# Three kinds of work change hands around the graphs that run ahead: row sums to a tile of their own, two evictions to ScalarE, half of the copies to VectorE

## The chip, the cores and the metric

The kernel runs on one core of a Trainium2 chip. A core has five engines with an instruction queue each: TensorE (PE in the profile, PEld for its weight loads), VectorE (DVE), ScalarE (ACT), GpSimd (POOL) and SyncE (SP), which here only issues transfers. Each queue is worked off in order, and engines wait for each other by semaphores. The metric is the device time of one execution in microseconds. Before the change it was 2126.53 us (median of 4 runs, 2122.99 to 2128.66).

## The reference, cut to what matters

There are 64 graphs of 256 nodes with 256 features, and two layers. What each computes:

```python
# layer 0, for each graph
deg = adjacency_matrix.sum(axis=-1);  deg = where(deg != 0, deg, 1.0)
a_plus = deg**-0.5 [:, None] * adjacency_matrix * deg**-0.5 [None, :] + max(alpha, 1e-10) * eye
x = layernorm(x + (a_plus @ x) @ W.T + b)
# layer 1, for each graph
h = relu(bn(conv1d(x.T, conv1_w, 0)))
h = bn(conv1d(h, conv2_w, 8))            # 17 taps along the nodes
x_conv = relu(h + x.T).T
s = x @ w_se.T + b_se                    # 3 numbers per node
dist = |s_n|^2 + |s_m|^2 - 2 s_n . s_m;  A = exp(-dist) * mask   # mask is adj
x_nmp = A @ relu(x @ w_msg.T + b_msg)
gi = concat(x_conv, x_nmp) @ w_ih.T + b_ih;  gh = x @ w_hh.T + b_hh
r, z = sigmoid(gi_r + gh_r), sigmoid(gi_z + gh_z);  n = tanh(gi_n + r * gh_n)
x = layernorm(x + (1 - z) * n + z * x)
```

Everything is float32.

## The kernel before, in words

The 64 graphs are worked in 4 groups (Q = 16 graphs each). For each group there are three kinds of work.

The **graph stages**: `layer0(g)` computes the first layer of a graph, and `layer1(g)` its second layer up to the gates. In `layer0`, `degrees()` (lines 354 to 359) sums the rows of the adjacency tile `a_t` on ScalarE: an activation that copies `a_t` and leaves the row sum in `deg` as accumulator output. The copy itself is not used. It is written into the tile `adjT`, which line 379 then overwrites with the transposed adjacency. From `deg`, VectorE and GpSimd make `dis` (power -1/2, line 369), ScalarE scales x with it into `x1` (line 391), and two VectorE operations put the diagonal into `adjT` (line 381). `adjT` has 3 buffers, and a buffer is free again when the multiplication at line 508 of three graphs before has read it.

`x1_transposed(g)` transposes x1 by TensorE into a PSUM bank and evicts it into `xn`: VectorE takes the first half (line 430, with a scale and a bias per partition, which put ones into the place of one channel), ScalarE the second (line 431). `layer1` multiplies it with the first convolution's weights (`p_conv`, line 446). ScalarE evicts that into `h` and `scols`, then come `p_msg` (467), the transform of h along the nodes (`p_dft`, 482, evicted into the tile V of all graphs of a group, line 487), the transposed distance columns `p_rows` (495), evicted as `dist_l` by ScalarE (497) and `dist_r` by VectorE (499), the distances `p_dist` (506), their exponential (507, ScalarE), the product with adjT (508, VectorE) and `p_nmp` (515). TensorE's order in a graph's turn is `p_rows`, `p_hT` of layer 0 two graphs ahead (399), `p_dist`, `p_out` (409), the transposes for the next graph's `xn`, `p_nmp`, then the next graph's `p_conv`, `p_adjT` (378), `p_msg` and `p_dft`.

The **convolution of a group** in the frequency domain: `products` (line 541, TensorE, weights streamed from memory) and then the inverse transform, `real_transform`, `complex_begin` and `complex_end`, all on VectorE, in place in the tile V/M; its results leave by the transfers of line 729.

The **gates** of a group's graphs: `gru(g)` (`p_g`, line 856), with their inputs loaded back from memory into tiles of the pool `gate`.

The groups overlap. While TensorE multiplies and VectorE transforms group 0, the first 12 graphs of group 1 (16 to 27) are already worked: AHEAD is 12, and the set ALONE holds exactly these graphs, beside which no gates run. For graphs in ALONE the transposes of the next graph's x1 are issued early, ahead of `p_nmp` (lines 510 and 511). The tile V is still in use then, so their transforms go into a second tile, V2. When `complex_end` has finished and its results have left, `copies` (lines 1080 to 1087) brings each graph's part from V2 to V, one copy of 128 x 768 elements per graph, on ScalarE. Then V2's memory is given back and the pool `gate` opens. For groups 1 and 2 AHEAD is 6, and gates of the group before run beside the graphs.

What comes before what on a queue is decided by a scheduler at build time, from the order in which the program issues the work and from the dependencies; `paced` ties steps of the VectorE transform to marked instructions of the graphs.

Of the kernel before, what the change touches and what calls it, by code (L numbers as in the profile page):

```python
# [9 lines left out]
F32 = mybir.dt.float32  # L10
AF = mybir.ActivationFunctionType
ALU = mybir.AluOpType
AX = mybir.AxisListType

P = 128
# [11 lines left out]
def kernel(  # L27
# [27 lines left out]
    nc = tc.nc  # L55
    B, N, D = x.shape
# [8 lines left out]
    GT = N // NT  # L65
# [6 lines left out]
    const = ctx.enter_context(tc.tile_pool(name="const", bufs=1))  # L72
# [9 lines left out]
    def bank(name):  # L82
        return ps.tile([P, 512], F32, tag="bank", name=name)
# [7 lines left out]
    def mark(op, gates=0):  # L91
        marks.append((op.ins, gates))
# [24 lines left out]
    alpha_t = const.tile([P, 1], F32)  # L117

    vectors = const.tile([16, P], F32, name="bn_in")
    neg_half = const.tile([P, 4], F32)  # L120
    nc.vector.memset(neg_half, -0.5)
    load(0)
# [17 lines left out]
    unit, others_only = ident[:, 0:1], const.tile([P, 1], F32, name="others_only")  # L140
# [177 lines left out]
    def layernorm(y, eps=LN_EPS):  # L318

        chunks = range(y.shape[1])  # L320
        st = small.tile([P, NCH, nc.vector.BN_STATS_DIM], F32, name="ln_st")
        mv = small.tile([P, NCH, nc.vector.BN_AGGR_DIM], F32, name="ln_mv")
        rs = small.tile([P, NCH], F32, name="ln_rs")
        for c in chunks:
            nc.vector.bn_stats(st[:, c, :], y[:, c, :])  # L325
            nc.vector.bn_aggr(mv[:, c, :], st[:, c, :])
        nc.vector.tensor_scalar(rs[:, : len(chunks)], mv[:, : len(chunks), 1], eps, None, op0=ALU.add)  # L327
        nc.gpsimd.tensor_tensor(rs[:, : len(chunks)], rs[:, : len(chunks)], neg_half[:, : len(chunks)], op=ALU.pow)  # L328
        yield
        mr = small.tile([P, NCH], F32, name="ln_mr")  # L330
        nc.vector.scalar_tensor_tensor(mr[:, : len(chunks)], mv[:, : len(chunks), 0], -1.0, rs[:, : len(chunks)], op0=ALU.mult, op1=ALU.mult)  # L331
        for c in chunks:
            nc.scalar.activation(  # L333
                y[:, c, :], y[:, c, :], AF.Identity, bias=mr[:, c : c + 1], scale=rs[:, c : c + 1]
            )
# [6 lines left out]
    ALONE = set()  # L342
# [3 lines left out]
    def layer0(g):  # L346

        a_t, x_t = ain.pop(g), xin.pop(g)

        adjT = work.tile([P, NCH, 3, P], F32, name="adjT", bufs=3)  # L350
        ADJT[g] = adjT

        deg = small.tile([P, NCH], F32, name="deg")
        def degrees():
            for c in range(NCH):
                nc.scalar.activation(
                    adjT[:, c, 0:2, :].rearrange("p n q -> p (n q)"), a_t[:, c, :], AF.Copy,
                    accum_out=deg[:, c : c + 1],
                )

        if g == 1:

            with tc.issue_after(X_SCALED[0]):
                degrees()
        else:
            degrees()
        nc.vector.scalar_tensor_tensor(deg, deg, 0.0, deg, op0=ALU.is_equal, op1=ALU.add)  # L367
        dis = small.tile([P, NCH], F32, name="dis")
        nc.gpsimd.tensor_tensor(dis, deg, neg_half[:, :NCH], op=ALU.pow)  # L369
        adeg = small.tile([P, NCH], F32, name="adeg")  # L370
        nc.vector.tensor_scalar(adeg, deg, alpha_t, None, op0=ALU.mult)

        p = bank("p_adjT").rearrange("p (c n) -> p c n", c=NCH)
        for mc in range(NCH):
            for c in range(NCH):
                nc.tensor.transpose(p[:, mc, c * P : (c + 1) * P], a_t[:, c, mc * P : (mc + 1) * P], ident)
        copied = nc.scalar.copy(adjT[:, :, 0:3:2, :], p.rearrange("p c (n q) -> p c n q", q=P))
        for mc in range(NCH):  # L380
            DIAGONAL[g] = nc.vector.scalar_tensor_tensor(
                adjT[:, mc, 1, :], ident, adeg[:, mc : mc + 1], adjT[:, mc, 2 * mc, :],
                op0=ALU.mult, op1=ALU.add,
            ).ins


        x1 = work.tile([P, NCH, D], F32, name="x1")
        X1[g] = x1
        with tc.issue_after(copied.ins) if g < 2 else ExitStack():
            for c in range(NCH):  # L390
                X_SCALED[g] = nc.scalar.activation(x1[:, c, :], x_t[:, c, :], AF.Copy, scale=dis[:, c : c + 1]).ins
        nc.gpsimd.tensor_tensor(x_t, x_t, b0_t.unsqueeze(1).to_broadcast([P, NCH, D]), op=ALU.add)

        yield
        hT = work.tile([P, DCH, N], F32, name="hT", bufs=1)
        p = bank("p_hT").rearrange("p (k n) -> p k n", k=DCH)
        for k in range(DCH):
            for mc in range(NCH):
                nc.tensor.matmul(  # L399
                    p[:, k, :], x1[:, mc, k * P : (k + 1) * P],  # L400
                    adjT[:, mc, 1 - mc : 3 - mc, :].rearrange("p n q -> p (n q)"),
                    start=mc == 0, stop=mc == NCH - 1,
                )
        nc.scalar.copy(hT, p)  # L404
        yield
        p = bank("p_out0").rearrange("p (c o) -> p c o", c=NCH)
        for c in range(NCH):
            for k in range(DCH):
                nc.tensor.matmul(  # L409
                    p[:, c, :], hT[:, k, c * P : (c + 1) * P], w0[:, k, :], start=k == 0, stop=k == DCH - 1  # L410
                )
        for c in range(NCH):
            mark(
                nc.vector.scalar_tensor_tensor(
                    x1[:, c, :], p[:, c, :], dis[:, c : c + 1], x_t[:, c, :], op0=ALU.mult, op1=ALU.add
                )
            )
        yield
        yield from layernorm(x1)
        nc.scalar.dma_start(x1_d[g // Q][g % Q].rearrange("(c p) d -> p c d", p=P), x1)  # L420
        yield

    def x1_transposed(g):
        x1 = X1.pop(g)
        xn = XN[g] = work.tile([P, 2 * DCH, N], F32, name="xn")
        p = bank("p_x1T").rearrange("p (k n) -> p k n", k=DCH)
        for k in range(DCH):
            for c in range(NCH):
                nc.tensor.transpose(p[:, k, c * P : (c + 1) * P], x1[:, c, k * P : (k + 1) * P], ident)
        nc.vector.tensor_scalar(xn[:, 0], p[:, 0], others_only, unit, op0=ALU.mult, op1=ALU.add)  # L430
        nc.scalar.copy(xn[:, 2 * DCH - 1], p[:, 1])

    def layer1(g, place):

        if g not in XN:
            x1_transposed(g)
        xn, adjT = XN.pop(g), ADJT.pop(g)
# [5 lines left out]
        for c in range(NCH):  # L443
            p = bank("p_conv1")[:, : D + NSE]
# [19 lines left out]
        p = bank("p_msg").rearrange("p (c d) -> p c d", c=NCH)  # L464
# [12 lines left out]
        for k in range(DCH):  # L477
            p = bank("p_dft")
# [14 lines left out]
        p = bank("p_rows")  # L493
# [2 lines left out]
        dl = work.tile([64, N], F32, name="dist_l", bufs=1)  # L496
        nc.scalar.copy(dl, p[0:64, :N])
        dr = work.tile([64, N], F32, name="dist_r", bufs=1)
        nc.vector.tensor_copy(dr, p[64:P, :N])
        yield  # L500

        aT = work.tile([P, NCH, 2, P], F32, name="aT", bufs=1)
        for c in range(NCH):
            rows = slice(32 * c, 32 * c + 32)
            p = bank("p_dist")[:, :N]
# [2 lines left out]
        mark(nc.vector.tensor_mul(aT, aT, adjT[:, :, 0:3:2, :]))  # L508
        yield
        if g in ALONE:  # L510
            x1_transposed(g + 1)
        p = bank("p_nmp").rearrange("p (k n) -> p k n", k=DCH)
        for k in range(DCH):
            for mc in range(NCH):
# [12 lines left out]
    V, M = VM.rearrange("p f (k q) -> p f k q", k=DCH), VM  # L527
# [447 lines left out]
    def graphs(first, part, others):  # L975


        for i in part:
            load(first + i + 3)
            given = {"layer0": layer0(first + i + 2) if first + i + 2 < B else iter(()), "other": others[i]}  # L980
            for piece, _ in enumerate(layer1(first + i, i)):
                if piece == APPLIED:
                    run(ENDS.pop())
                    ENDS.append(given["layer0"])
                elif piece == STATS:
                    next(given["layer0"], "end")
                yield
                for name in PLACES[piece]:
                    if next(given[name], "end") != "end":
                        yield  # L990
            yield from given["other"]
# [59 lines left out]
    def open_ahead(graphs):  # L1051

        scope = ExitStack()
        pool = scope.enter_context(tc.tile_pool(name="ahead", bufs=1))
        return scope, graphs, pool.tile([P, FL, DCH, graphs * GT], F32, name="V2")
# [23 lines left out]
    scope, AHEAD, V2 = open_ahead(12)  # L1079
    def copies(V2):  # L1080

        waiting = list(AWAY)
        AWAY.clear()
        TILES[0] = V
        for i in waiting:
            nc.scalar.copy(V[:, :, :, i * GT : (i + 1) * GT], V2[:, :, :, i * GT : (i + 1) * GT])
            yield

    late = nothing()
    for q in range(NQ):  # L1090
# [32 lines left out]
        if more:  # L1123
# [9 lines left out]
            if q == 0:  # L1133
                scope, AHEAD, V2 = open_ahead(6)
# [58 lines left out]
```

## Time and profile before

| | |
|---|---|
| median of 4 runs | 2126.53 us |
| the profiled execution's own time | 2126.25 us |
| its span in the profile | 2124.5 us |
| PE busy | 2003.0 us, 94% |
| DVE busy | 1471.5 us, 69% |
| ACT busy | 904.3 us, 43% |
| POOL busy | 663.5 us, 31% |

The profile shows one execution. Busy time is summed over instructions that are at work; an engine that waits is not busy. The waits table says for which instruction an engine waited and for how long. The granted clock is TensorE's clock as a share of full speed. The timeline gives start and duration of instructions, merged when equal ones follow each other, and in brackets the idle time before them and what ended it.

### The profile page before, as it was taken

The page shows a single profiled execution, that of the slowest core. Times are in us where ns is not written, and L with a number is a line of the kernel's source. Part 1 is how long each engine was busy: PE and PEld are TensorE (multiplying, and loading weights), DVE is VectorE, ACT ScalarE, POOL GpSimd, SP SyncE. Part 2 cuts the span into 40 slices and gives each one's busy share as a digit, 9 for nine tenths or more (in the row PEclk, how much of TensorE's full clock was granted, in tenths as well). Part 3 has the DMA queues.
Part 4 walks back from the last instruction along what each step waited for, and adds up shares of the span by engine and source line. Part 5 has one row for each costly group of instructions (what it writes and reads, how often), then busy time and mean ns, then how long its engine had stood idle before and what let it go on. Part 6 is the DMA issues. An engine that isn't in the chain of part 4 may idle for free. (4 is left out here: it accounts for less than half of the span.)

```text
span 2124.5 us, 26260 instructions
## 1 busy us (share of the span) xinstructions
PE 2003.0 (94%) x8157; PEld 1440.6 (68%) x8157; DVE 1471.5 (69%) x3347; ACT 904.3 (43%) x2114; POOL 663.5 (31%) x672
## 2 busy tenths in 40 slices
PE   6999999888999999999999999999999999899997
PEld 4888888766667766667767765667767765555554
DVE  5555567775558788774456888875444889976776
ACT  4666643456432234556453223446544123333333
POOL 3445310121431243313322234323222123344443
PEclk9999999999999999999999999999999999999999
DMA  4766656433337644344335754334323844444331
GB/s 125 230 209 199 195 180 213 154 129 122 112 99 224 198 129 134 119 114 119 95 105 156 220 155 136 122 108 135 95 85 93 259 139 139 110 115 98 93 97 55
DMA packets 305289, 298.05 MB, mean 140 GB/s; under 512 B 84192, under 2 KB 283956, under 8 KB 305150
## 3 DMA queue, kind: packets, MB, share of 16 engines
q1 hardware_dynamic: 245198, 200.37, 32.3%
q10 hardware_dynamic: 44480, 67.39, 8.9%
q0 software_dynamic: 15472, 28.61, 6.0%
q8 instruction: 66, 1.08, 0.2%
q14 instruction: 73, 0.60, 0.1%
HBM read 193.19 MB, written 103.06 MB: 139 GB/s over the span
## 5 line engine op out<-in xcount | busy, mean ns | idle before, releaser
L856 PE MATMUL p_g<-wall,sums 128*128 128x384 f32 x1536 | 537.0, 489 | 10.4 <-DVE G L882 10.2
L856 PE MATMUL p_g<-wall,inputs 128*128 128x384 f32 x1152 | 406.5, 489 | 13.5 <-DVE G L874 13.4
L856 PEld LDWEIGHTS p_g<-wall,sums 128*128 128x128 f32 x1536 | 284.0, 190 | 199.2 <-issue 19.6
L856 PEld LDWEIGHTS p_g<-wall,inputs 128*128 128x128 f32 x1152 | 217.4, 190 | 165.4 <-DVE G L874 22.1
L838 POOL TENSOR_TENSOR sums<-inputs 128x384 f32<-128x384 f32 x128 | 139.4, 1090 | 344.9 <-PE p_g L856 298.3
L369 POOL TENSOR_TENSOR dis<-deg,neg_half 128x2 f32<-128x2 f32 x64 | 48.4, 756 | 481.9 <-DVE deg L367 478.0
L897 ACT ACTIVATE G<-G 128x512 f32<-128x512 f32 x128 | 80.6, 630 | 245.6 <-DVE G L884 144.4
L328 POOL TENSOR_TENSOR ln_rs<-ln_rs,neg_half 128x2 f32<-128x2 f32 x129 | 94.9, 736 | 271.5 <-DVE ln_rs L327 226.1
L541 PE MATMUL p_k<-u,VM 128*128 128x256 f32 x736 | 174.9, 380 | 3.2 <-DMA u<-ud 3.2
L541 PEld LDWEIGHTS p_k<-u,VM 128*128 128x128 f32 x736 | 138.9, 190 | 29.7 <-DMA u<-ud 3.9
L446 PE MATMUL p_conv<-wc,xn 128*128 128x259 f32 x512 | 129.7, 390 | 23.0 <-DVE xn L430 21.8
L399 PE MATMUL p_hT<-adjT,x 128*128 128x256 f32 x512 | 127.8, 393 | 15.6 <-ACT msg L470 8.1
L508 DVE TENSOR_TENSOR aT<-aT,adjT 128x512 f32<-128x512 f32 x64 | 45.5, 711 | 126.8 <-ACT aT L507 126.5
L333 ACT ACTIVATE x_g<-x_g,ln_mr,ln_rs 128x256 f32<-128x256 f32 x128 | 70.0, 593 | 148.2 <-DVE ln_mr L331 145.8
L446 PEld LDWEIGHTS p_conv<-wc,xn 128*128 128x128 f32 x512 | 93.8, 191 | 53.5 <-DVE xn L430 31.6
L409 PE MATMUL p_out<-w,hT 128*128 128x256 f32 x512 | 125.1, 388 | 3.6 <-ACT hT L404 3.2
L482 PE MATMUL p_dft<-fwd,h 128*128 128x240 f32 x512 | 117.5, 372 | 11.5 <-ACT scols L450 11.1
L515 PE MATMUL p_nmp<-aT,msg 128*128 128x256 f32 x512 | 121.5, 380 | 0.7 <-DVE aT L508 0.7
L467 PE MATMUL p_msg<-wmsg,xn 128*128 128x256 f32 x512 | 121.4, 380 | 0.0
L331 DVE SCALAR_TENSOR_TENSOR ln_mr<-ln_mv,ln_rs 128x2 f32<-128x2 f32 x129 | 47.3, 368 | 103.9 <-POOL ln_rs L328 103.9
L409 PEld LDWEIGHTS p_out<-w,hT 128*128 128x128 f32 x512 | 96.4, 192 | 31.2 <-ACT hT L404 12.0
L399 PEld LDWEIGHTS p_hT<-adjT,x 128*128 128x128 f32 x512 | 95.1, 196 | 32.4 <-ACT msg L470 9.8
(160 smaller groups left out, 3612.0 us busy)
## 6 DMA issues: line engine op xcount, KB each, us to landing
u<-ud SPq DMA_DIRECT2D x284, 256.0 KB
xn_d<-xn ACTq DMA_DIRECT2D x64, 512.0 KB
inputs<-xn_d SPq DMA_DIRECT2D x64, 512.0 KB
ud<-u_set POOLq DMA_DIRECT2D x39, 480.0 KB, 6.3
adj_t<-in_adj_dram SPq DMA_DIRECT2D x64, 256.0 KB
x_t<-in_x_dram SPq DMA_DIRECT2D x64, 256.0 KB
x_d<-x ACTq DMA_DIRECT2D x64, 256.0 KB
xc_d<-VM SPq DMA_DIRECT2D x64, 256.0 KB
```

What stands on the lines that cost most here:

```text
L328: nc.gpsimd.tensor_tensor(rs[:, : len(chunks)], rs[:, : len(chunks)], neg_half[:, : len(chunks)], op=ALU.pow)
L333: nc.scalar.activation(y[:, c, :], y[:, c, :], AF.Identity, bias=mr[:, c : c + 1], scale=rs[:, c : c + 1])
L399: nc.tensor.matmul(p[:, k, :], x1[:, mc, k * P : (k + 1) * P], adjT[:, mc, 1 - mc : 3 - mc, :].rearrange("p n q -> p (n q)"), start=mc == ...
L409: nc.tensor.matmul(p[:, c, :], hT[:, k, c * P : (c + 1) * P], w0[:, k, :], start=k == 0, stop=k == DCH - 1)
L446: nc.tensor.matmul(p, x1T[:, k, c * P : (c + 1) * P], wc1[:, k, :], start=k == 0, stop=k == DCH - 1)
L467: nc.tensor.matmul(p[:, c, :], x1T[:, k, c * P : (c + 1) * P], wmsg[:, k, :], start=k == 0, stop=k == DCH - 1)
L482: nc.tensor.matmul(p[:, t0 * FL : t1 * FL], h[:, c, k * P : (k + 1) * P], fwd[:, first : first + t1 - t0, :].rearrange("p t f -> p (t f)") ...
L515: nc.tensor.matmul(p[:, k, :], msg[:, mc, k * P : (k + 1) * P], aT[:, mc].rearrange("p n q -> p (n q)"), start=mc == 0, stop=mc == NCH - 1,)
L541: nc.tensor.matmul(p[:, j * D : (j + 1) * D], v[:, k, :], u[:, k, :], start=k == 0, stop=k == DCH - 1)
L838: nc.gpsimd.tensor_tensor(S[i], x, y, op=op)
L856: nc.tensor.matmul(p[:, : 3 * HD] if k == 0 else p[:, HD:], a[:, k], wall[:, b, k].rearrange("p t d -> p (t d)"), start=first and k == 0, ...
L897: nc.scalar.activation(rz, rz, AF.Tanh, scale=0.5)
```

## The change

Four edits. `degrees()` writes its unused copy into a constant tile `unused` (128 x 256) instead of `adjT`; this concerns all 64 graphs. For the graphs that follow one in ALONE (17 to 28), the first half of `xn` is evicted by ScalarE, as an Identity activation with the same scale and bias, instead of VectorE. For the 12 graphs in ALONE, `dist_r` is evicted by ScalarE instead of VectorE. The copies from V2 to V go to VectorE for every second graph. Nothing changes on TensorE but some places in its order.

```diff
+    unused = const.tile([P, N], F32, name="unused")
...
                 nc.scalar.activation(
-                    adjT[:, c, 0:2, :].rearrange("p n q -> p (n q)"), a_t[:, c, :], AF.Copy,
+                    unused, a_t[:, c, :], AF.Copy,
                     accum_out=deg[:, c : c + 1],
                 )
...
-    def x1_transposed(g):
+    def x1_transposed(g, alone=False):
...
-        nc.vector.tensor_scalar(xn[:, 0], p[:, 0], others_only, unit, op0=ALU.mult, op1=ALU.add)
+        if alone:
+            nc.scalar.activation(xn[:, 0], p[:, 0], AF.Identity, bias=unit, scale=others_only)
+        else:
+            nc.vector.tensor_scalar(xn[:, 0], p[:, 0], others_only, unit, op0=ALU.mult, op1=ALU.add)
         nc.scalar.copy(xn[:, 2 * DCH - 1], p[:, 1])
...
-        nc.vector.tensor_copy(dr, p[64:P, :N])
+        if g in ALONE:
+            nc.scalar.copy(dr, p[64:P, :N])
+        else:
+            nc.vector.tensor_copy(dr, p[64:P, :N])
...
         if g in ALONE:
-            x1_transposed(g + 1)
+            x1_transposed(g + 1, True)
...
         for i in waiting:
-            nc.scalar.copy(V[:, :, :, i * GT : (i + 1) * GT], V2[:, :, :, i * GT : (i + 1) * GT])
+            copy = nc.vector.tensor_copy if i % 2 else nc.scalar.copy
+            copy(V[:, :, :, i * GT : (i + 1) * GT], V2[:, :, :, i * GT : (i + 1) * GT])
             yield
```

The build of the changed kernel shows how the scheduler then orders the queues. The row sums move forward on ScalarE: before, a graph's pair stood behind the exponentials (507) of the graph three before, whose product (508) frees the adjT buffer; now it stands somewhere between the eviction of `p_msg` (470) and the exponentials, mostly around the evictions of `p_dft` (487) and `dist_l` (497). On VectorE and GpSimd `deg` and `dis` move forward with them. Behind the exponentials of a graph in ALONE, ScalarE now does both evictions of the next `xn`, then mostly both scalings of x (391), then the eviction of `p_nmp` (519). Of the copies for group 1, six stand on each engine in one row; for groups 2 and 3, five copies are made each time, three on ScalarE and two on VectorE. Of the transfers, SyncE's order changes at one place only, where two loads of the gates' inputs change places with another.

## The prediction

> **What bounds the kernel now.** I read the page's busy table first, then TensorE's waits, then busy times by stage, then the timeline where the waits lie. TensorE (PE) is the bound on average:
>
> ```profile
> PE 2003.0 (94%) x8157; PEld 1440.6 (68%) x8157; DVE 1471.5 (69%) x3347; ACT 904.3 (43%) x2114; POOL 663.5 (31%) x672
> ```
>
> So time can only be won where PE idles, some 121 us of the span. The windows of the stage in which graphs 16 to 28 run ahead (columns: stretch, length, then busy time and count of PE, PEld, DVE, ACT, POOL, granted clock, DMA share, GB/s):
>
> ```profile
> 282.00:391.00 109.00, 108.05 (x522) 92.77 (x520) 81.91 (x183) 39.37 (x96) 11.50 (x12) 1.00 0.70 220
> 391.00:513.40 122.40, 106.10 (x519) 84.98 (x518) 94.48 (x266) 66.35 (x183) 22.57 (x24) 1.00 0.36 120
> 513.40:538.00 24.60, 15.60 (x63) 12.24 (x61) 7.40 (x26) 17.54 (x36) 5.55 (x7) 0.86 0.52 140
> 538.00:560.00 22.00, 21.76 (x85) 14.85 (x86) 7.35 (x14) 10.50 (x27) 9.71 (x10) 1.00 0.35 91
> ```
>
> Up to 391 us PE is full (convolution products). From 391 to 513 it idles 16.3 us while DVE is 77% busy and ACT 54%. From 513 to 538 it idles 9.0 us, the clock falls to 0.86, and ACT is the busiest engine: 1.2% of the span holds 7% of the idle time. PE's waits from 391 to 540 us (what waited, for what, total, times, longest):
>
> ```profile
> PE p_conv L446 <- DVE xn L430: 12.6, 8, 3.1
> PE p_dft L482 <- ACT scols L450: 6.1, 1, 6.1
> PE p_hT L399 <- DVE adjT L381: 3.2, 4, 1.5
> PE p_dist L506 <- DVE dist_r L499: 1.8, 3, 1.1
> ```
>
> Three of these four go through instructions that the change moves. In the timeline the 6.1 us wait is ACT's row of copies, and what follows is slow:
>
> ```profile
> 514.28 0.83 ACT L1086 COPY VM<-V 128x768 f32<-128x768 f32 x1
> 515.02 8.16 ACT L1086 COPY VM<-V 128x768 f32<-128x768 f32 x11
> 515.55 1.89 PE L467 MATMUL p_msg<-wmsg,xn 128*128 128x256 f32 x8
> 523.08 0.37 ACT L449 ACTIVATE h<-p_conv 128x256 f32<-128x256 f32 x1
> 523.56 3.57 PE L482 MATMUL p_dft<-fwd,h 128*128 128x240 f32 x8 [6.12 <-ACT scols L450]
> ```
>
> `h` is evicted only behind the last copy. And this is a usual turn, where xn waits behind eight DVE operations of the inverse transform and of x though its transposes were done at 438.54:
>
> ```profile
> 437.94 0.60 PE L429 MATMUL p_x1T<-ident,x 128*128 128x128 f32 x4
> 441.83 0.54 DVE L430 TENSOR_SCALAR xn<-p_x1T,others_only,ident 128x256 f32<-128x256 f32 x1
> 442.40 0.37 ACT L431 COPY xn<-p_x1T 128x256 f32<-128x256 f32 x1 [1.51 <-DVE xn L430]
> 442.42 1.61 PEld L446 LDWEIGHTS p_conv<-wc,xn 128*128 128x128 f32 x8 [2.55 <-DVE xn L430]
> ```
>
> **The change part by part**, against the profiled execution's own 2126.25 us (span 2124.5, 1.75 around it), which stands 0.3 below the median of the four runs: no correction.
>
> *xn to ScalarE (12 graphs).* Removed from DVE: 12 x 0.54 us. Added to ACT: an activation from PSUM with two per-partition operands. No row has that; from below 0.38 us (relu of p_conv, PSUM, no such operand), from above 0.61 (the normalising activation, SBUF, two); I take 0.57, as one such operand raises the PSUM row to 0.47 (exponential). ACT's queue there: the exponentials end at 436.94, the transposes at 438.54, so both halves would be in place by about 438.6 + 0.57 + 0.37 = 439.5, ahead of p_nmp's end at 440.3. The wait goes. In 391 to 513 it is 3.07 + 0.22 + 2.15 + 0.19 + 1.49 + 1.59 + 0.93 = 9.6 us (the eighth, 2.92, is at 538). What is late next: the chain through DVE of adjT's diagonal (waits 3.2), of nsq and of the masked product, since each turn's DVE work shrinks only by 0.97 us of about 11. A faster turn calls it earlier. Queued behind the new ACT instruction are the scalings of x and the eviction of p_nmp; ACT now idles 1.7 us before the latter, so 0.57 fits. Ends: -1 us (12 x 0.1, if the ACT instruction were on the path and slower) and +9.6. I take two thirds, 6.4, for DVE keeps its 77%.
>
> [...] I think that the queue decides here, not the operation.
>
> *dist_r to ScalarE (12).* DVE's 0.43 goes, ACT gets about 0.36 (dist_l's row) behind dist_l. It no longer waits behind transform operations: PE's waits for it, with those before 391 counted, are 0.39 + 0.52 + 0.33 + 1.06 + 0.39 = 2.7 us. Behind it on ACT stands hT's eviction, which idles 2.4 us before its start (435.48), so that cover holds 0.36 easily; without it 12 x 0.36 = 4.3 would be lost. Ends 0 and +2.7; I take +2.0.
>
> *Row sums to their own tile (64 graphs).* Same operations, same size. Removed: ACT's wait for the masked product, 36.1 us in 43 places, at which ACT had nothing urgent. Moved forward: 0.91 us of ACT per graph, two small DVE operations and the 0.71 us power on POOL; its POOL neighbour, the 1.4 us sum of x and b0, comes after. No transfer moves: the adjacency tile was loaded about 20 us before it is read (issue 428.6, read in 452.7). Gain bound: the wait for the diagonal, all over the kernel 5.1 us, say +3. Loss bound: outside ALONE one half of the pair (0.46) now stands ahead of an eviction of p_dft or of dist_l for 52 graphs, where TensorE already waits (8.1 for msg's bank, 2.2 for dist_l, 1.1 for p_dft's bank). If a quarter show it, 52/4 x 0.46 = 6. p_hT (1.9 us) runs meanwhile and covers most. I take -1.
>
> *Copies of group 1.* ACT's row falls from 8.9 us (514.28 to 523.18) to 0.83 + 5 x 0.74 = 4.5. `h` follows 4.4 us sooner, and the 6.1 us stall becomes 1.7. DVE's six have no row of their kind: above 0.96 each (between a 128x512 product at 0.69 and a 128x1024 one at 1.30, linear), below 0.43 (the 64x256 copy); both sums, 2.6 to 5.8 us, end by about when scols is ready for DVE (4.5 + 1.0), where it idled 8.4 us before. So the price is 0; at the upper end 0.3. The slow clock after the stall: p_dft 3.57 for a usual 1.78, p_rows 0.64 for 0.38, p_hT 2.98 for 1.97, together 3.06 us. After the 3.07 us stall at 398 p_conv took the usual 2.02, so a stall of 1.7 should not bring it. [...] I take 4.4 + 3.0 = 7.4 (ends 4.1 and 9.2).
>
> *The turn after it.* p_conv at 538.08 waited 2.92 because xn stood behind ln_mr on DVE, which waited for POOL's power. In the new order xn stands ahead of both, but behind a 0.70 us block transposition, which waits for a load. The gate tiles lie in V2's memory, so these loads start when the last copy ends (523.20 before, about 4.4 sooner now, as does everything around). Ends 0 and +2.4; I take 1.5.
>
> *Copies of groups 2 and 3.* Five each; DVE takes two. PE's waits around are 0.59 (p_dist on p_dft's bank) and 0.5. Ends: -3.8 (4 x 0.96 on DVE) and +1.1; I take 0.5.
>
> Sum: 6.4 + 2.0 - 1 + 7.4 + 1.5 + 0.5 = 16.8; 2126.25 - 16.8 = 2109.5, forecast 2110. Downstream PE is 96% busy (560 to 1640), so what it starts sooner it ends sooner.
>
> **The rivals.**
> A. *DVE becomes the bound while graphs run ahead.* For it: 77% busy, in order, POOL stretches its operations (one of 0.4 us took 1.50 at 504.71), and the copies can't start before its last transform step. Against: it loses 12 us of work with the waits. Then only the copies (7.4) and a little remain: 2126.25 - 8 = 2118.
> B. *The gain is absorbed.* After 520 the gates' loads decide, not TensorE. For: their first load is issued at 523.20, with the last copy. Against: they are released by the copies, which end sooner too. 2126.
> C. *Slower: the row sums hold up evictions.* If the half pair (0.46) ahead of p_dft's and dist_l's evictions came onto TensorE's path for all 52 graphs outside ALONE, it would cost 23.9: 2126.25 - 17.8 + 23.9 = 2132. It decides from 17.8 / 0.46 = 39 graphs on. For: these evictions free PSUM banks that TensorE waited for. Against: ACT is 43% busy, and p_hT covers about 1.9 us.
>
> **How the numbers follow.** Forecast 0.65, A 0.19, B 0.07, C 0.09. The largest gains sum to 9.6 + 2.7 + 3 + 9.2 + 2.4 + 1.1 = 28 (2098); not all come together, so the range starts at 2101. Above, it goes past A by its own uncertainty to 2122, leaving B and C out. A measurement here tells about 0.2% (4.3 us) from no change, so forecast and A are faster, B the same, C slower: 0.84, 0.07, 0.09.
>
> **What would show it.** The wait of p_conv for xn in 391 to 513 falls from 9.6 below 4 us; p_dist's for dist_r vanishes; six copies on ACT in 4.5 us and p_dft behind a stall under 2.5 us at 1.8 us length, clock near 1.0. Wrong, if waits for adjT, scols or the masked product rise by as much (A), if the stage 513 to 560 keeps its length (B), or if p_hT and p_dist wait tens of us more for msg, VM or dist_l (C).

## The result, and the profile after

The changed kernel took 2135.23 us (median of 53 runs, 2120.48 to 2148.64) beside 2130.25 us for the kernel before (median of 78 runs): a ratio of 1.0023, with a 95% interval of 1.0014 to 1.0032. It is slower by a little, where 2110 us and a gain were forecast. The profiled execution took 2135.12 us with a span of 2133.3 us, so it stands for the median. In the code after, the lines behind the first edit have numbers up to 8 higher (the row sums are line 357, `p_dist` is 513, the copies are 1094).

The engines' busy times hardly move, as the page's busy table of the changed kernel shows:

```profile
PE 2009.6 (94%) x8157; PEld 1445.9 (68%) x8157; DVE 1472.9 (69%) x3333; ACT 905.2 (42%) x2128; POOL 669.7 (31%) x672
```

TensorE is busy 6.6 us longer with the same 8157 instructions, which is slow clock (0.988 on average, 0.992 before), and idle 2.2 us longer. To see where, I cut both traces at the four places where a group's products begin (`p_real` on TensorE), and did the same later for two of the experiments:

| stage (us) | before | changed | without row sums | row sums held |
|---|---|---|---|---|
| start to 1st products | 283.08 | 295.50 | 283.94 | 283.32 |
| to 2nd (graphs ahead, copies) | 353.79 | 332.84 | 336.23 | 330.09 |
| to 3rd | 504.20 | 519.04 | 504.65 | 511.57 |
| to 4th | 501.06 | 504.78 | 501.22 | 505.01 |
| to the end of the span | 482.37 | 481.14 | 482.46 | 480.71 |

The stage at which three of the four edits are aimed is 21.0 us shorter. The gain is there, but 12.4, 14.8 and 3.7 us are lost in the first, third and fourth stage, and with 1.2 us won at the end the span is 8.8 us longer. In these three stages nothing has changed but the row sums and, in the third and fourth, two copies each that went to VectorE. The last stage holds none of the instructions that the edits change. In the thirteen traces of this document it is 477.1 to 486.2 us long, so a few microseconds in one stage of one trace can be chance.

The waits table of before (what waited, for what, total us, times, longest) has these lines:

```profile
ACT adjT L356 <- DVE aT L508: 36.1, 43, 3.5
...
PE p_conv L446 <- DVE xn L430: 21.8, 20, 3.1
...
PE p_dist L506 <- DVE dist_r L499: 4.1, 8, 1.1
```

In that of the changed kernel the first two lines below are new or much larger, and the third, of x1 transposed, is smaller:

```profile
ACT unused L357 <- DMA adj_t<-in_adj_dram: 46.1, 29, 5.1
...
PE p_dist L513 <- DVE dist_r L506: 14.6, 13, 2.9
PE p_conv L450 <- DVE xn L434: 14.6, 14, 2.4
```

Before, ScalarE's row sums waited 36.1 us for the masked product and its table has no line of them for their own load. Now they wait 46.1 us in 29 places for the transfer of their adjacency tile. `p_dist` waited 4.1 us before and now waits 14.6. The timeline of the changed kernel shows the one going over into the other:

```profile
231.79 0.37 SPq L108 DMA_DIRECT2D adj_t<-in_adj_dram  x1
...
234.34 0.48 ACT L491 COPY VM<-p_dft 128x384 f32<-128x384 f32 x1 [0.21 <-PE p_dft L486]
238.33 0.42 ACT L357 ACTIVATE unused<-adj_t 128x256 f32<-128x256 f32 x1 [3.52 <-DMA adj_t<-in_adj_dram]
...
238.75 0.46 ACT L491 COPY VM<-p_dft 128x384 f32<-128x384 f32 x1
239.11 0.36 ACT L501 COPY dist_l<-p_rows 64x256 f32<-64x256 f32 x1
...
239.50 0.43 DVE L506 COPY dist_r<-p_rows 64x256 f32<-64x256 f32 x1 [5.44 <-ACT dist_l L501]
...
239.98 0.70 PE L513 MATMUL p_dist<-dist_r,dist_l 32*128 32x256 f32 x4 [2.92 <-DVE dist_r L506]
...
240.61 3.69 PE L308 MATMUL p_u<-taps,dft_w 85*120 85x256 f32 x8
```

Read it from the top. The tile's load is issued at 231.79. The sum of its rows is next on ScalarE at 234.8 and has to wait until 238.33. Behind it in the queue stand the second eviction of `p_dft` and that of the left rows, which have nothing to do with the load. VectorE's right rows wait for these, and TensorE stops for 2.92 us. After that the clock falls too: the granted clock is 0.59 from 240 to 244 us and 0.56 from 244 to 248, and the eight `p_u` products take 3.69 us, where they take 1.99 before (at 234.33).

In the third stage there is also a stall of another kind: in the timeline `p_g` at 692.26 waits 2.99 us for VectorE and then runs at slow clock. Which part of the change brings that one is not visible in the trace.

The three other edits look as forecast. The copies, in the timeline of the changed kernel:

```profile
512.12 0.84 ACT L1094 COPY VM<-V 128x768 f32<-128x768 f32 x1
512.86 3.76 ACT L1094 COPY VM<-V 128x768 f32<-128x768 f32 x5
513.40 2.89 DVE L1094 COPY VM<-V 128x768 f32<-128x768 f32 x6
...
517.01 1.89 PE L486 MATMUL p_dft<-fwd,h 128*128 128x240 f32 x8 [1.49 <-ACT scols L454]
```

The stall is 1.49 us instead of 6.12, and `p_dft` behind it runs at full speed. In the stretches, TensorE idles 2.6 us around the copies instead of 9.0 and 4.1 us in the stretch before them instead of 16.3, though the stretches are cut a little differently (columns as in the prediction):

```profile
403.00:511.60 108.60, 104.55 (x516) 85.61 (x516) 83.60 (x249) 74.92 (x197) 24.10 (x24) 1.00 0.40 136
511.60:536.00 24.40, 21.82 (x98) 16.10 (x97) 11.36 (x32) 16.82 (x40) 9.93 (x11) 1.00 0.64 176
```

### The profile page after: what moved, and what is told of

Same layout as the page of the kernel before. It is cut to its first block, busy times and chain, and to the rows that moved or that the text cites. A ratio compares the mean times of both kernels' runs of the same rounds, so it can differ in the third digit from the quotient of the medians.

```text
span 2133.3 us, 26191 instructions
## 1 busy us (share of the span) xinstructions
PE 2009.6 (94%) x8157; PEld 1445.9 (68%) x8157; DVE 1472.9 (69%) x3333; ACT 905.2 (42%) x2128; POOL 669.7 (31%) x672
## 5 line engine op out<-in xcount | busy, mean ns | idle before, releaser
L863 PE MATMUL p_g<-wall,inputs 128*128 128x384 f32 x1152 | 410.0, 492 | 17.6 <-DVE G L881 15.3
L863 PEld LDWEIGHTS p_g<-wall,inputs 128*128 128x128 f32 x1152 | 218.0, 191 | 170.5 <-DVE G L881 24.3
L548 PEld LDWEIGHTS p_k<-u,VM 128*128 128x128 f32 x736 | 140.2, 192 | 30.5 <-DMA u<-ud 3.6
L450 PE MATMUL p_conv<-wc,xn 128*128 128x259 f32 x512 | 127.2, 387 | 15.8 <-DVE xn L434 14.6
L400 PE MATMUL p_hT<-adjT,x 128*128 128x256 f32 x512 | 128.2, 393 | 12.7 <-ACT msg L474 8.7
L370 POOL TENSOR_TENSOR dis<-deg,neg_half 128x2 f32<-128x2 f32 x64 | 46.1, 720 | 293.2 <-DVE deg L368 287.9
L393 POOL TENSOR_TENSOR x_t<-x_t,b_t 128x512 f32<-128x512 f32 x64 | 94.4, 1475 | 134.9 <-issue 110.6
L450 PEld LDWEIGHTS p_conv<-wc,xn 128*128 128x128 f32 x512 | 94.3, 190 | 44.6 <-DVE xn L434 22.9
L845 POOL TENSOR_TENSOR sums<-inputs,sums 128x384 f32<-128x384 f32 x64 | 69.4, 1085 | 155.7 <-PE p_g L863 155.0
```

What stands on the lines that cost most here:

```text
L400: nc.tensor.matmul(p[:, k, :], x1[:, mc, k * P : (k + 1) * P], adjT[:, mc, 1 - mc : 3 - mc, :].rearrange("p n q -> p (n q)"), start=mc == ...
L450: nc.tensor.matmul(p, x1T[:, k, c * P : (c + 1) * P], wc1[:, k, :], start=k == 0, stop=k == DCH - 1)
L548: nc.tensor.matmul(p[:, j * D : (j + 1) * D], v[:, k, :], u[:, k, :], start=k == 0, stop=k == DCH - 1)
L845: nc.gpsimd.tensor_tensor(S[i], x, y, op=op)
L863: nc.tensor.matmul(p[:, : 3 * HD] if k == 0 else p[:, HD:], a[:, k], wall[:, b, k].rearrange("p t d -> p (t d)"), start=first and k == 0, ...
```

## The experiments

Three theories were told apart. **W**: the row sums, no longer held by an adjT buffer, are ordered so early that they wait at the head of ScalarE's queue for their own load, and what stands behind them holds TensorE. **P**: the load costs nothing; the 0.91 us of ScalarE work that now stands ahead of the evictions does (this is the prediction's rival C). **N**: the row sums are harmless, and the gain of the other edits is lost somewhere else (rival B in spirit).

**Row sums alone**: the kernel before with the first edit only.

```diff
-                    adjT[:, c, 0:2, :].rearrange("p n q -> p (n q)"), a_t[:, c, :], AF.Copy,
+                    unused, a_t[:, c, :], AF.Copy,
```

> Only the row sums' own tile is added to the kernel before. Theory W (the row sums, set free, are issued a graph's turn earlier, stand at the head of ScalarE's queue until their own adjacency tile has landed, and the evictions behind them hold TensorE): slower than before by 15 to 25 us, about 2145 to 2155, with some 30 us or more of ScalarE waiting for the DMA of the adjacency tile. Theory P (only the 0.9 us of ScalarE work per graph, now in front of evictions, costs time, the load does not): also slower, by about 15 to 20 us. Theory N (the row sums' place costs nothing, and the gain of the three other edits is lost somewhere else): within 4 us of before.

Measured: 2160.57 us, ratio 1.0144 (1.0127 to 1.0160), slower by 30.7 us, a little past the upper end. Its waits:

```profile
ACT unused L357 <- DMA adj_t<-in_adj_dram: 43.5, 30, 5.2
...
PE p_dist L507 <- DVE dist_r L500: 15.2, 15, 3.0
```

The same two lines as in the changed kernel, so they come from this edit. N falls.

**Without the row sums' edit**: the three other edits on the kernel before.

> The changed kernel without the row sums' own tile: x1 transposed, right rows and copies as changed. Theories W and P: faster than before by 12 to 20 us, about 2110 to 2118, near the forecast of 2110 less its 1 us for the row sums. Theory N: 2128 to 2137, no faster than before.

Measured: 2110.32 us, ratio 0.9902 (0.9886 to 0.9919). That is 20.9 us faster, and the time that was forecast for the whole change. Beside its trace, TensorE in the changed kernel idles 17.9 us longer and is busy 6.9 us longer at a lower clock. `p_dist`'s wait for the right rows is down to these lines:

```profile
PE p_dist L512 <- DVE dist_r L505: 1.4, 3, 0.8
...
PE p_dist L512 <- ACT dist_r L503: 0.6, 1, 0.6
```

**Row sums held**: the changed kernel, with one order on ScalarE's queue. `EXPS[g]` is the last exponential of graph g.

```diff
-            degrees()
+            with tc.issue_after(EXPS[g - 3]) if g > 2 else ExitStack():
+                degrees()
```

> The changed kernel with one order added on ScalarE: the row sums of a graph are issued only after the exponentials of the graph that layer 1 works on in that turn, which is the place they have in the kernel before. Theories W and P: ScalarE's wait for the adjacency tile is gone and the time is 2108 to 2118. Theory N: 2130 to 2137, as the changed kernel.

Measured: 2115.45 us, ratio 0.9927 (0.9910 to 0.9943). The row sums still write to their own tile; only their place in the queue is the old one. ScalarE's wait for the adjacency tile is gone from the waits table, and some 20 of the 26 us are back. So the place is the cause of most of the loss. About 5 us against the run without the row sums' edit are left.

**Three adjacency tiles**: the changed kernel with loads a turn earlier, meant to take the wait and leave the place. The diff leaves out two lines that make room for the buffer: the tile `unused` is bf16, and a tile of the setup, `diagonal`, has one buffer.

```diff
-        ain[g] = loads.tile([P, NCH, N], F32, name="adj_t")
+        ain[g] = loads.tile([P, NCH, N], F32, name="adj_t", bufs=3)
```

> The changed kernel with a third buffer for the adjacency tile, so that each is loaded a turn earlier, while the row sums stay at nearly the early places they have in the changed kernel (to make room, the tile that the row sums write is bf16 and the diagonal of the setup has one buffer). Theory W: ScalarE's wait for the adjacency tile goes from 46 us to under 10 and the time to 2110 to 2120. Theory P: the wait goes but the time stays at 2130 to 2137, since the 0.9 us of ScalarE still stand before the evictions. Theory N: 2130 to 2137 as well, and the two runs before tell it from P.

Measured: 2132.62 us, ratio 1.0013 (0.9997 to 1.0028), no gain. But this is not what P expects either, for the wait did not go:

```profile
ACT unused L357 <- DMA adj_t<-in_adj_dram: 39.6, 29, 4.4
```

and in its timeline the sums are again right behind their load:

```profile
235.20 0.37 SPq L108 DMA_DIRECT2D adj_t<-in_adj_dram  x1
...
241.68 0.42 ACT L357 ACTIVATE unused<-adj_t 128x256 bf16<-128x256 f32 x1 [3.46 <-DMA adj_t<-in_adj_dram]
```

The sums have simply moved forward by another graph's turn: ahead of the message eviction of graph k, in most turns of the traces, ScalarE has done the sums of graphs up to k+2 in the kernel before, k+3 in the changed one and k+4 here. With a third buffer, too, a free row sum follows its load.

**Three tiles, row sums behind the message eviction**: the test, mended. `MSGS[g]` is the eviction of `p_msg` of graph g, which stands ahead of those of `p_dft`. The same two lines for room are left out.

```diff
-        ain[g] = loads.tile([P, NCH, N], F32, name="adj_t")
+        ain[g] = loads.tile([P, NCH, N], F32, name="adj_t", bufs=3)
...
-            degrees()
+            with tc.issue_after(MSGS[g - 3]) if g > 2 else ExitStack():
+                degrees()
```

> The run with three adjacency tiles did not make the test it was meant for: the row sums were issued earlier still, and again right behind their load. Here the changed kernel has three adjacency tiles (the row sums' tile is bf16 and the setup's diagonal has one buffer, as there), and the row sums are held behind the message eviction of the graph that layer 1 works on in that turn: they stand where the changed kernel has them within a turn, ahead of the evictions of p_dft, of the left rows and of hT, but their tile was loaded a turn earlier. Theory W (the wait for the load): no wait for the adjacency tile on ScalarE, and 2110 to 2120. Theory P (the 0.9 us of ScalarE ahead of the evictions): no wait either, but 2126 to 2137.

Measured: 2116.55 us, ratio 0.9946 (0.9932 to 0.9959). Its timeline has the sums where the changed kernel has them in a turn, between the evictions, but a turn later than there. The pair that is read at 236.09 was loaded from 201.90 on, and there is no wait:

```profile
235.72 0.48 ACT L495 COPY VM<-p_dft 128x384 f32<-128x384 f32 x1 [0.21 <-PE p_dft L490]
236.09 0.42 ACT L358 ACTIVATE unused<-adj_t 128x256 bf16<-128x256 f32 x1
...
236.53 0.48 ACT L495 COPY VM<-p_dft 128x384 f32<-128x384 f32 x1
236.90 0.36 ACT L505 COPY dist_l<-p_rows 64x256 f32<-64x256 f32 x1
237.17 0.42 ACT L358 ACTIVATE unused<-adj_t 128x256 bf16<-128x256 f32 x1
```

W expected 2110 to 2120, P 2126 to 2137. The same ScalarE work ahead of the same evictions cannot be told in time from the held run with the old place (0.9946 beside 0.9927, each good to about 0.0015), and 16 of the 26 us are back; it was the wait for the load that cost them, and P falls as the main cause. A price of a few microseconds for the place is not excluded: against the run without the row sums' edit (0.9902) this one is 9.4 us slower. About 5 of these stand in the held run as well, and for 1.5 us TensorE waits for the setup's single `diagonal`, which neither the kernel before nor the held run has.

**Parts of the gain.** Four runs split the other edits. Only the copies:

> Only the copies from V2 to V are shared by the two engines, the rest is the kernel before. By the prediction's terms (7.4 and 0.5 us, and 1.5 us in the turn after): faster by 7 to 10 us, a ratio of 0.9955 to 0.9965. If the gain is put back by later waits: within 3 us of before.

Measured: 2120.11 us, ratio 0.9961 (0.9946 to 0.9976), 8.3 us, as expected. Only x1 transposed and the right rows, both for the graphs ahead:

> Only x1 transposed and the right rows go to ScalarE in the graphs ahead, the rest is the kernel before. By the prediction's terms (6.4 and 2.0 us): faster by 6 to 10 us, a ratio of 0.9953 to 0.9972; without_row_sums was 20 us faster, so that what is left over from copies_alone should be here: 10 to 13 us.

Measured: 2119.76 us, ratio 0.9959 (0.9945 to 0.9974), 8.7 us: within the prediction's terms, less than the 10 to 13 that were left over. Then each of the two by itself:

> Only x1 transposed of the graphs ahead goes to ScalarE. By the prediction's term: 6.4 us faster (its ends were 1 us slower and 9.6 us faster), a ratio of 0.997. If the term is right and that of the right rows too small, it stays at 5 to 7 us here.

> Only the right rows of the graphs ahead go to ScalarE. By the prediction's term: 2.0 us faster (its ends were 0 and 2.7 us), a ratio of 0.999, which is no difference that the runs can tell. If the 9 us of the two edits together come from here as well: 3 us or more.

Measured: x1 transposed 2125.05 us, ratio 0.9967 (0.9954 to 0.9980), 7.0 us faster, where 6.4 was expected. Right rows 2122.88 us, ratio 0.9952 (0.9937 to 0.9967), 10.2 us, against 2.0. That is a miss, and not explained: in its trace the stage with the graphs ahead is shorter by 3.1 us only (350.7 for 353.8; TensorE idles 4.2 us less in it and is busy 1.1 us longer), 4.9 us are won in the last stage, which the edit does not touch, and `p_conv` still waits 20.1 us for xn:

```profile
PE p_conv L446 <- DVE xn L430: 20.1, 17, 2.9
```

Either edit takes work from VectorE in the same turns, and together they give no more than one gives; the intervals of the three runs (4.3 to 9.8 us for x1, 7.0 to 13.4 for the right rows, 5.5 to 11.7 for both) overlap. By the profiles the stage is 4.1 us shorter with x1 alone, 3.1 with the right rows alone, 8.1 with both and 11.0 with the copies; all three together give 17.6. By the stage the terms add up roughly (4.1 and 3.1 for 8.1, 8.1 and 11.0 for 17.6); the timed 10.2 us of the right rows alone stay open.

**x1 transposed by ScalarE for all graphs**, a way on that the waits suggested: without the row sums' edit, TensorE still waited 12.7 us in 12 places for VectorE's xn.

```diff
         if g not in XN:
-            x1_transposed(g)
+            x1_transposed(g, True)
```

> The changed kernel without the row sums' own tile, and with x1 transposed evicted by ScalarE for all graphs, not only those that run ahead. In without_row_sums TensorE still waits 12.7 us in 12 pieces for VectorE's x1 transposed. If those waits end with ScalarE's 0.56 us: 2098 to 2108. If ScalarE's queue is late in those stages (it is 43% busy, and the evictions of h come behind): 2108 to 2118, no better than without_row_sums.

> Only x1 transposed goes to ScalarE, and for all graphs. x1_by_scalar_everywhere was 15.6 us faster than without_row_sums. If that gain stands by itself and x1 transposed of the graphs ahead is worth 6.4 us: 20 to 24 us faster than before, 2105 to 2109. If it rests on the copies and the right rows: 8 to 14 us faster.

Measured: with the copies and the right rows 2094.74 us, ratio 0.9840 (0.9827 to 0.9853); alone 2100.84 us, ratio 0.9857 (0.9837 to 0.9876), 30.5 us. Both are faster than was expected of them, and the first is the fastest version found: 34 us below the kernel before. TensorE's wait for xn in it, and the busy table, on which VectorE has 39.9 us less than before and ScalarE 25.6 more:

```profile
PE 1997.1 (95%) x8157; PEld 1444.1 (69%) x8157; DVE 1431.6 (68%) x3281; ACT 929.9 (44%) x2180; POOL 662.5 (32%) x672
```

```profile
PE p_conv L449 <- ACT xn L431: 7.2, 8, 1.2
```

Compared with the run without the row sums' edit, 4.9, 6.5 and 10.0 us of this come in the first, third and fourth stage (279.03, 498.20 and 491.21 us long), while its second stage is 3.6 us and its last 2.3 us longer. So ScalarE's queue was free enough in those three stages as well.

## Why the prediction was wrong

**The row sums.** This is the term that failed. It was set at -1 us, with ends of -6 and +3; with the three other edits in place it measures about -26 (ratio 1.0023 less 0.9902, of 2130 us), by itself -30.7. The failing sentence is "No transfer moves: the adjacency tile was loaded about 20 us before it is read". It used the slack of the old place for the new one. The profile of before had most of what was needed:

```profile
220.37 0.42 ACT L356 ACTIVATE adjT<-adj_t 128x256 f32<-128x256 f32 x1
...
228.56 0.38 SPq L108 DMA_DIRECT2D adj_t<-in_adj_dram  x1
...
231.86 0.48 ACT L487 COPY VM<-p_dft 128x384 f32<-128x384 f32 x1 [0.33 <-PE p_dft L482]
...
236.02 0.42 ACT L356 ACTIVATE adjT<-adj_t 128x256 f32<-128x256 f32 x1
...
251.41 0.42 ACT L356 ACTIVATE adjT<-adj_t 128x256 f32<-128x256 f32 x1 [0.76 <-DVE aT L508]
```

The pair that is read at 251.41 was loaded from 228.56 on, 22.9 us ahead; a turn in that stage takes 15.65 us (220.37 to 236.02). The new order puts the pair a whole graph's turn earlier and, within the turn, from behind the exponentials to ahead of the second eviction of `p_dft`, which is another 4.2 us (231.86 to 236.02). So 22.9 - 15.65 - 4.2 = 3.1 us are left, and the load takes 6.5 (231.79 to 238.33 in the trace after): a wait of 3.4 us, and the trace after has 3.52. I had read the place within the turn off the new order, but not whose turn it was. The removed wait of 36.1 us was rightly called harmless (the run without the row sums' edit keeps 35.0 us of it and gains), and just that made it valuable: at the place where nothing urgent stood, it kept the row sums from waiting at a worse one.

**Rival C** named the place ("the row sums hold up evictions") and came out near in time, 2132 for 2135, with the wrong price: 0.46 us of work on each of 52 graphs, 23.9 us in all. The run with the sums between the evictions and their tile loaded leaves a few microseconds for that price at most; what cost was up to 5.1 us of waiting in 29 places. So its time is near by luck. It had a chance of 0.09, and the range up to 2122 left it out.

**x1 transposed**: 6.4 forecast, 7.0 alone. ScalarE's activation was put at 0.57 us and takes 0.564, where VectorE's operation took 0.536. The forecast that the wait in that stretch falls below 4 us holds: in the changed kernel none is left from 403 to 513, and 0.6 us in the turn after. The prediction's view that the queue decides and not the operation is borne out: the kernel that moves all 64 to ScalarE is the faster by 30.5 us. In its trace TensorE's wait for xn is 6.2 us instead of 21.8, though the operation is the longer one there too (0.566 us): TensorE had waited for VectorE's queue and not for the operation. That is half of the gain; where the rest comes from was not separated.

**Right rows**: 2.0 forecast. With x1 transposed beside it, both gave 8.7 for a sum of 8.4; alone it measured 10.2, which I can't account for. `p_dist`'s wait did not vanish as forecast either: from 403 to 513 it waits 1.4 us for the right rows, now on ScalarE.

**Copies and the turn after**: 7.4 + 1.5 + 0.5 = 9.4 forecast, 8.3 measured alone (interval 5.1 to 11.5), 11.0 in its profile's stage. The stall became 1.49 us (1.7 was forecast) and the six copies on VectorE took 0.55 us each, within the bounds of 0.43 and 0.96 (a line between the two rows that the prediction names gives 1.00, not 0.96).

**The sum without the row sums** was 17.8 us. The run without them gained 20.9 (17.3 to 24.3). So the sum of the other five terms stood, though not each size: the right rows alone missed theirs, and the turn after the copies and the copies of groups 2 and 3 were not measured apart. The slack of one load decided the sign.

**Rival A** (VectorE becomes the bound) and **rival B** (absorbed) are both excluded by that run: the stage kept 17.6 us of the gain and gave less than 1 us back behind it.

Open are three things: some 5 us between the run with the row sums held (0.9927) and the one without their edit (0.9902), whose intervals overlap (in the held one's trace the third stage is 6.9 us longer, with longer waits of `p_dft` for scols, the fourth 3.8 us longer and the second 6.1 us shorter); the stall of `p_g` at 692 us in the changed kernel's trace; and the 10.2 us of the right rows alone.

## What to carry to other kernels

Before a wait is removed because nothing urgent stands behind it, work out where the freed instruction will go: the scheduler here moved it forward to the next thing it depends on, its own load, and at the head of an in-order queue it then held up whatever stood behind it there (here by up to 5.1 us at a time). Subtract the distance it moves, in whole turns and within the turn, from the slack its inputs had at the old place. When an engine's result is late because of its queue, moving the operation to a less loaded queue can pay even if it is slower there (here 0.566 us for 0.536), and it is worth asking at once where else in the kernel the same wait stands: the edit made for 12 graphs was worth 7 us, for all 64 it was worth 30.

## What the hardware showed that was not expected

The granted clock did not follow the length of the stall. TensorE ran at full speed after stalls of 1.49 us (the changed kernel, 517.01: `p_dft` in 1.89 us), 1.71 us (copies alone, 521.17: 1.89 us) and 3.07 us (before, 398.25: `p_conv` in the usual 2.02), but at about half after 2.92 us (the changed kernel, 239.98: a granted clock of 0.50 from 240.73 on) and 2.99 us (692.26: 0.50 from 691.29 on), and even after 2.30 us, as this line of the run without the row sums' edit shows, where 1.89 us is the full-speed time:

```profile
513.90 3.46 PE L485 MATMUL p_dft<-fwd,h 128*128 128x240 f32 x8 [2.30 <-ACT scols L453]
```

The clock records of two traces, without the first 40 and the last 20 us, show what it followed. In the kernel before the clock falls at 270.13, 522.72, 590.99, 1430.67 and 1748.11, which is 74, 20, 246 and 93 times 3.413 us from one to the next. In the changed kernel it falls at 240.73, 578.65, 609.37, 691.29, 923.40, 1032.62, 1213.53 and 1548.04: 99, 9, 24, 68, 32, 53 and 98 times 3.413 us. It stays at 0.50 for 6.83 us after 522.72 in the first and after 240.73 and 691.29 in the second, and for 3.41 us after the ten others. Cut into stretches of that length, the run without the row sums' edit has (columns as in the prediction):

```profile
510.31:513.72 3.41, 1.29 (x6) 0.79 (x5) 2.07 (x5) 3.41 (x7) 0.00 (x0) 1.00 0.58 192
513.72:517.13 3.41, 3.23 (x8) 2.75 (x9) 1.03 (x5) 3.20 (x10) 1.27 (x1) 0.50 0.40 64
```

and the kernel before, around its stall of 3.07 us, with the cuts counted back from its fall at 522.72:

```profile
393.01:396.42 3.41, 2.17 (x13) 1.62 (x10) 3.38 (x6) 1.20 (x5) 0.00 (x0) 1.00 0.00 0
396.42:399.84 3.42, 1.59 (x7) 1.37 (x8) 2.92 (x12) 0.41 (x2) 0.78 (x2) 1.00 0.73 230
399.84:403.25 3.41, 3.41 (x19) 3.04 (x19) 1.94 (x6) 3.00 (x9) 1.86 (x2) 1.00 0.25 77
```

The shorter stall lay almost wholly within one stretch (511.60 to 513.90), in which TensorE was busy for 1.29 us, and the next stretch was at half clock. The longer one was split over two stretches with 2.17 and 1.59 us of work, and the clock stayed. In the traces of the kernel before and of the changed one, cut so throughout, twelve of the thirteen falls follow a stretch at full clock in which TensorE was busy for 1.45 us or less, and the thirteenth one with 1.84 us (575.24 to 578.65 in the changed kernel). No stretch at full clock with less than 1.53 us of work is without a fall behind it.

So the prediction's reason for 3.0 us of clock gain ("After the 3.07 us stall at 398 p_conv took the usual 2.02, so a stall of 1.7 should not bring it") does not hold, and that the outcome was as forecast is in part luck: the stall of 1.49 us left 1.92 us of work in its stretch (513.80 to 517.21), little more than the 1.84 us behind which the clock fell elsewhere in the same trace, and in the run without the row sums' edit the slow clock came back. My estimate from these rows: a stall that leaves a stretch of 3.41 us with 1.45 us of work or less costs itself plus some 1.6 us for each stretch at half clock (3.46 us for 1.89 above). After the stall of 2.92 us there were two of them, from 240.73 to 247.56; why one or two follow is not shown.
